# A four-layer graph network on one core: layer 3's first chunk moved into the last attention head

## The chip, the cores and the metric

The kernel runs on one core of a Trainium2 chip. Its time is the device time of one launch in microseconds (us); lower is better. A profiled execution gives, for every instruction, when it started, how long it was busy and what its engine had waited for. The engines are TensorE (PE; PEld is its weight load), VectorE (DVE), ScalarE (ACT), GpSimd (POOL) and SyncE (SP), whose queue issues most of the DMAs.

## The reference, cut to what matters

A graph of N = 2708 nodes with D = 512 features passes through four layers, each on the layer norm and relu of x, and each added to x. Layer 2 is attention with H = 8 heads of O = 64 outputs, and an elu behind it; layer 3 is a mean over neighbours.

```python
# layer 2, h = relu(layernorm(x))
Wh = einsum('nd,hdo->hno', h, W)
e = leaky_relu(f1[:, :, None] + f2[:, None, :], 0.2)
attention = softmax(where(adj > 0, e, NEG_INF), axis=-1)
x = x + elu(einsum('hnm,hmo->hno', attention, Wh))
# layer 3, h = relu(layernorm(x))
agg = mask @ h / maximum(deg, 1.0)
combined = concatenate([h @ W_self + b_self, agg @ W_nb + b_nb], axis=-1)
x = x + relu(combined @ W_comb + b_comb)
```

## The kernel before, in words

Nodes are cut into NC = 22 **chunks** of R = 128 rows (the last has 20). The two matrices of layer 3 are multiplied with W_comb beforehand (`fused`), so a chunk of layer 3 needs two products of 512 by 512: `nb3` (what the neighbours will be given, split into a high and a low half by `halves`) and `self3` (its own share plus a bias b3, sent to DRAM as s3). Then every chunk is summed over its neighbours (`aggregate`).

The attention runs as 220 **steps** in one loop. A step is one chunk of neighbours m for one head or half head ("unit"); the first and the last head are cut in two by columns, and the last unit covers columns 1408 to 2707. I number the 22 steps of this last unit 0 to 21; in the code they are steps 198 to 219. In a step s

- `make` (VectorE, L1066) writes the weights t of the step, 128 x 1300 here, into a tile "t2" (TILES = 4 buffers); the loop calls it three steps ahead;
- `scale` (ScalarE, L1051 and L1053) writes whs: the chunk's values wh and a column of ones, both times a factor of each row, also three steps ahead, in 4 buffers;
- `multiply` (TensorE, L1266) multiplies the two into "av" (eight matmuls) and "sums" (four).

After a unit, `evict` copies av and sums to SBUF (ScalarE) and to DRAM as avT and sumT (SP's queue). Layer 3 starts by reading them back. Its steps for a chunk c are

- `load3`: aT (256 KB) and sT (40 KB) from avT and sumT, and x2 (256 KB), all on SP's queue;
- `turn3`: a small product with `mix` and four transposes (TensorE), four 8-wide operations that end with a reciprocal (VectorE, L1221 to L1224), and y = av times the reciprocal, one 128 x 512 operation of VectorE (L1226);
- `elu3`: z = min(y, 0) (GpSimd, L1233), x + max(y, 0) (VectorE), tanh and exp of z (ScalarE, L1236 and L1237, with a table load between them), their product (VectorE, L1238), and its addition to x (VectorE, L1239);
- `save3`: x to DRAM on ScalarE's queue;
- `normalize3`: statistics of x (VectorE), a root (ScalarE, L223, with a table load), its reciprocal, and hn = (x - mean) * rs (VectorE, L234). `norm` has a second form, `scalar=True`, in which VectorE makes a one-element shift and ScalarE writes hn (L231);
- `transpose3`: four transposes of hn (TensorE, L245) and a relu to hT (ScalarE, L247);
- then `nb3` and `self3`.

The author plans what runs beside the attention with `behind(s, fn, c)`: fn is called at the end of step s. The tile framework then orders the instructions of each engine itself and puts in the waits; each engine executes its list strictly in that order. Before, the plan puts chunk 0's steps up to `transpose3` and parts of chunks 1 to 4 into steps 6 to 21 of the last unit; nb3 and self3 of all chunks follow after the loop:

```python
        for c in range(NC):
            nb3(c)
            if c:
                do(transpose3, c + 1)
            do(turn3, c + 3)
            do(normalize3, c + 2)
            do(save3, c + 2)
            do(elu3, c + 3)
            do(load3, c + 5)
            final = self3(c)
            if c == 0:
                transpose3(1)
```

Of the kernel before, what the change touches and what calls it, by code (L numbers as in the profile page):

```python
# [8 lines left out]
F32 = mybir.dt.float32  # L9
# [5 lines left out]
AF = mybir.ActivationFunctionType  # L15
ALU = mybir.AluOpType
# [4 lines left out]
P = 128  # L21

R = 128
# [3 lines left out]
TILES = 4  # L27
# [17 lines left out]
def fast_layers(  # L45
# [36 lines left out]
    nc = tc.nc  # L82
    N, D = x_in.shape
    H, _, O = w2.shape
    NC = -(-N // R)
# [6 lines left out]
    def rows(c):  # L92
        return min(R, N - c * R)

    def move(engine, dst, src):

        if dst.shape[0] == last_rows:
            cut = last_rows // 16 * 16
            engine.dma_start(dst[:cut], src[:cut])
            return engine.dma_start(dst[cut:], src[cut:])  # L100
        return engine.dma_start(dst, src)
# [21 lines left out]
    common = ctx.enter_context(tc.tile_pool(name="common", bufs=2))  # L123
# [84 lines left out]
    def any_product(c, po, lhsT, w, n):  # L208
        if c == NC - 1:
            product_of_last(po, lhsT, w)  # L210
        else:
            product(po, lhsT, w, n)
# [3 lines left out]
    def norm(xc, n, scalar=False):  # L216

        st = small.tile([P, nc.vector.BN_STATS_DIM], F32, name="ln_st")
        nc.vector.bn_stats(st[:n], xc[:n])  # L219
        mv = small.tile([P, nc.vector.BN_AGGR_DIM], F32, name="ln_mv")  # L220
        nc.vector.bn_aggr(mv[:n], st[:n])  # L221
        rs = small.tile([P, 1], F32, name="ln_rs")
        nc.scalar.activation(rs[:n], mv[:n, 1:2], AF.Sqrt, bias=eps[:n], scale=1.0)  # L223
        nc.vector.reciprocal(rs[:n], rs[:n])
        hn = common.tile([P, D], F32, name="hn", tag="t", bufs=3)
        if scalar:
            shift = small.tile([P, 1], F32, name="ln_shift")
            nc.vector.tensor_scalar(
                shift[:n], mv[:n, 0:1], rs[:n], -1.0, op0=ALU.mult, op1=ALU.mult
            )  # L230
            nc.scalar.activation(hn[:n], xc[:n], AF.Relu, bias=shift[:n], scale=rs[:n])  # L231
            return hn
        normed.append(
            nc.vector.tensor_scalar(  # L234
                hn[:n], xc[:n], mv[:n, 0:1], rs[:n], op0=ALU.subtract, op1=ALU.mult
            ).ins
        )
        return hn
# [89 lines left out]
    bias3 = dram.tile([1, D], F32, name="bias3")  # L328
# [641 lines left out]
    one6 = at.tile([R, S], F32, name="one6")  # L970
    nc.gpsimd.memset(one6, 0.0)
    nc.gpsimd.memset(one6[:, 6:7], 1.0)
    row, weight, wh, whs, acc, sides, made = {}, {}, {}, {}, {}, {}, []

    def load_row1(h, lo, hi):

# [79 lines left out]
    def make(s):  # L1056
        u, m = steps[s]
        h, lo, hi = units[u]
        q = rows(m)
        g, k = where[m]  # L1060
        if in_tails(u, m):
            weight[s] = tails_row[:LINES]
            made.append(made[-1])
            return
        t = at.tile([R, N], F32, name="t2", bufs=TILES)
        ins = nc.vector.scalar_tensor_tensor(  # L1066
            t[:q, : hi - lo],
            row[h][:q, lo:hi],
            ec[:q, m, h : h + 1],
            vT[g][:q, k, lo:hi],  # L1070
            op0=ALU.max,
            op1=ALU.mult,
        )
        weight[s] = t[:q]
        made.append(ins.ins)
# [114 lines left out]
    tails_w = tails.tile([P, len(middle), O + S], F32, name="tails_w")  # L1190
    nc.gpsimd.memset(tails_w, 0.0)
    tails_f = tails.tile([P, 3], F32, name="tails_f")
    kept3, l3_weights = {}, []


    def load3(c):
# [15 lines left out]
    def turn3(c):  # L1212
        xc, aT, sT = kept3[c]
        pr = ps.tile([P, 2, H], F32, name="sums_ps", tag="ps")
        nc.tensor.matmul(pr[:R], sT, mix[:NS], start=True, stop=True)
        pt = ps.tile([P, H, O], F32, name="av_ps", tag="ps")
        flat = pt.rearrange("p h o -> p (h o)")
        for k in range(NF):
            nc.tensor.transpose(flat[:R, k * P : (k + 1) * P], aT[:, k, :], ident)  # L1219
        rs = e3.tile([R, H, 1], F32, name="rs")  # L1220
        nc.vector.tensor_tensor(rs[:, :, 0], er[:, c], pr[:R, 0], ALU.mult)  # L1221
        nc.vector.tensor_tensor(rs[:, :, 0], rs[:, :, 0], pr[:R, 1], ALU.add)
        nc.vector.tensor_scalar(rs[:, :, 0], rs[:, :, 0], TINY, None, op0=ALU.max)
        nc.vector.reciprocal(rs[:, :, 0], rs[:, :, 0])  # L1224
        y = e3.tile([R, H, O], F32, name="y3")
        nc.vector.tensor_tensor(y, pt[:R], rs.to_broadcast([R, H, O]), ALU.mult)  # L1226
        kept3[c] = xc, y.rearrange("p h o -> p (h o)")

    def elu3(c):

        xc, y = kept3[c]
        z = e3.tile([R, D], F32, name="z3")
        nc.gpsimd.tensor_scalar(z, y, 0.0, None, op0=ALU.min)  # L1233
        nc.vector.scalar_tensor_tensor(xc[:R], y, 0.0, xc[:R], op0=ALU.max, op1=ALU.add)
        th = e3.tile([R, D], F32, name="th3", bufs=1)
        nc.scalar.activation(th, z, AF.Tanh, scale=0.5)  # L1236
        nc.scalar.activation(z, z, AF.Exp)  # L1237
        nc.vector.scalar_tensor_tensor(z, z, 1.0, th, op0=ALU.add, op1=ALU.mult)  # L1238
        nc.vector.tensor_tensor(xc[:R], xc[:R], z, ALU.add)  # L1239
        kept3[c] = xc  # L1240

    def save3(c):
        n = rows(c)
        move(nc.scalar, x3[c * R : c * R + n, :], kept3[c][0][:n])

    def normalize3(c):
        kept3[c] = kept3[c], norm(kept3[c], R)

    def transpose3(c):
        kept3[c] = kept3[c][0], relu_T(kept3[c][1], R)  # L1250
# [167 lines left out]
        behind(first + 2, count_neighbors, i)  # L1418

    for at_step, fn, c in (  # L1420
        (16, load3, 0),
        (15, load3, 1),
        (9, turn3, 0),
        (8, load3, 2),
        (8, elu3, 0),
        (6, normalize3, 0),
        (6, save3, 0),
        (6, turn3, 1),
        (5, load3, 3),
        (2, transpose3, 0),  # L1430
        (2, turn3, 2),
        (1, load3, 4),
    ):
        behind(len(steps) - at_step, fn, c)

    for s in range(len(steps)):
        if s == (len(units) - 3) * NC + 1:
            tails_ctx.close()
            e3_ctx = ctx.enter_context(ExitStack())
            e3 = e3_ctx.enter_context(  # L1440
                tc.tile_pool(name="e3", bufs=2, side="right", reuse_waits="tile")
            )
        if s + 6 < len(steps) and (s + 6) % NC % GROUP == 0:
            load_wh(s + 6)
        if s + 3 < len(steps):
            scale(s + 3)
            make(s + 3)
        if s + 1 < len(steps):
            compare(s + 1)
        multiply(s)  # L1450
        multiply_sides(s - 1)
        for fn, args in plan.pop(s, ()):
            if fn in (load_l3_weights, spread_nodes, split):
                with tc.issue_after(made[s]):
                    fn(*args)
            else:
                fn(*args)
# [4 lines left out]
    with ExitStack() as stack:  # L1462
        margin = stack.enter_context(tc.tile_pool(name="margin", bufs=1))
        margin.tile([P, 112], F32, name="margin")
        ring = stack.enter_context(tc.tile_pool(name="ring3", bufs=NC - 1, reuse_waits="tile"))
        b3 = ring.tile([P, D], F32, name="b3", bufs=1)
        nc.sync.dma_start(
            b3, bass.AP(tensor=bias3.tensor, offset=bias3.offset, ap=[[0, P], [1, D]])
        )
        h3 = {}  # L1470
        wself, wnb = l3_weights

        def nb3(c):
            pn = ps.tile([P, D], F32, name="nb3_ps", tag="ps")
            any_product(c, pn, kept3[c][1], wnb, R)
            h3[c] = halves(ring, pn, c)

        def self3(c):
            n = rows(c)
            po = ps.tile([P, D], F32, name="self_ps", tag="ps")  # L1480
            any_product(c, po, kept3.pop(c)[1], wself, R)
            y = common.tile([P, D], F32, name="y", tag="t", bufs=3)
            for own in corners if c == NC - 1 else [(slice(0, n), slice(0, D))]:
                ins = nc.vector.tensor_tensor(y[own], po[own], b3[own], ALU.add)
                move(nc.scalar, s3[c * R : c * R + n, own[1]], y[own])
            return ins.ins

        def do(fn, c):
            if c < NC:
                fn(c)  # L1490


        elu3(1)
        normalize3(1)
        save3(1)
        elu3(2)
        for c in range(NC):
            nb3(c)
            if c:
                do(transpose3, c + 1)  # L1500
            do(turn3, c + 3)
            do(normalize3, c + 2)
            do(save3, c + 2)
            do(elu3, c + 3)
            do(load3, c + 5)
            final = self3(c)
            if c == 0:
                transpose3(1)

        e3_ctx.close()  # L1510
        wk = stack.enter_context(
# [688 lines left out]
```

## Time and profile before

| what | us |
|---|---|
| median of 3 runs (1754.12 to 1757.56) | 1755.75 |
| the profiled execution's own time | 1757.88 |
| its span | 1756.1 |
| TensorE busy | 1728.0 |
| VectorE busy | 1307.0 |
| ScalarE busy | 850.1 |
| GpSimd busy | 248.0 |
| step 0 of the last unit starts on TensorE | 1315.7 |
| the last sums of the attention end | 1359.6 |
| nb3 of chunk 0 starts | 1359.5 |
| the last self3 ends and the aggregation begins, about | 1533 |

Times within the execution count from the start of the span. A line of the timeline gives start, duration, engine, line, operation, output<-inputs, shapes and count; a bracket at its end gives how long the engine was idle before it and which instruction ended that. TensorE's ends are modelled: a TensorE that is busy is not thereby at full speed, and the granted clock (1.00 is full) is read beside it.

### The profile page before, as it was taken

The numbers are of one execution on the slowest core, as the hardware profiler recorded it, in microseconds if no ns is written. First come the engines' busy times: TensorE is split into PE (matmuls) and PEld (weight loads), VectorE is DVE, ScalarE is ACT, GpSimd is POOL, SyncE is SP. The second block draws the span as 40 slices with busy tenths as digits, with TensorE's granted clock in tenths as the row PEclk, the third lists the DMA queues.
The fourth block names the chain that finished last, engine by engine and source line by source line (L and its number), as shares of the span: only waits on it lengthen the run. The fifth ranks groups of instructions, "written<-read, shape, count | busy, mean of one in ns | idle before, by whom it ended". The sixth has DMA issues, their size and how long they took to land.

```text
span 1756.1 us, 29494 instructions
## 1 busy us (share of the span) xinstructions
PE 1728.0 (98%) x11280; PEld 1050.8 (60%) x11280; DVE 1307.0 (74%) x1889; ACT 850.1 (48%) x1547; POOL 248.0 (14%) x252
## 2 busy tenths in 40 slices
PE   8999999999999999999999999999999999999998
PEld 5567777744468887644474554433434455588886
DVE  7759889855455557878699999999999777633334
ACT  5447777622210000365888888888794566400000
POOL 1003323311111112265000000000001222100000
PEclk9999999999999999999899999999999999999999
DMA  8436666444551112332420221122022444313221
GB/s 291 139 117 199 206 207 186 136 114 129 115 135 49 48 49 66 113 126 93 125 63 15 60 64 34 38 64 61 14 68 69 135 139 132 112 34 110 74 72 41
DMA packets 167227, 177.37 MB, mean 101 GB/s; under 512 B 84127, under 2 KB 106591, under 8 KB 166060
## 3 DMA queue, kind: packets, MB, share of 16 engines
q1 hardware_dynamic: 144428, 131.99, 27.1%
q10 hardware_dynamic: 18808, 33.37, 5.1%
q0 software_dynamic: 3840, 10.03, 1.5%
q8 instruction: 90, 1.47, 0.4%
q14 instruction: 61, 0.50, 0.1%
HBM read 111.64 MB, written 55.36 MB: 95 GB/s over the span
## 4 chain that ended last, share of the span: by engine, by line
PE 84%; DVE 9%; issue 2%; ACT 2%; DMA 1%; SPq 0%; POOL 0%; ACTq 0%; DVEq 0%; POOLq 0%
PE acc L424 36%; PE av L1266 15%; PE nb_ps L187 8%; DVE t L1066 6%; PE h_ps L187 4%; PE line_ps L187 4%; PE sums L1266 4%; PE self_ps L187 4%; PE hT_ps L245 2%; PE wh_ps L187 2%; PE fused_ps L370 2%; PE av_ps L1219 1%; PE adj_sums L1365 1%; ACT b L1084 1%; DVE kt L870 0%
## 5 line engine op out<-in xcount | busy, mean ns | idle before, releaser
L1066 DVE SCALAR_TENSOR_TENSOR t<-rb,ec,vT 128x2708 f32<-128x2708 f32 (+2 forms) x214 | 510.7, 2453 | 19.5 <-PE sums L1266 17.8
L1266 PE MATMUL av<-t,whs 128*32 128x451 f32 (+5 forms) x4432 | 431.1, 514 | 4.4 <-DVE t L1066 1.4
L424 PE MATMUL acc<-halves,kt 128*128 128x512 f32 x1848 | 426.4, 391 | 2.4 <-DVE kt L870 2.1
L424 PEld LDWEIGHTS acc<-halves,kt 128*128 128x128 f32 x1848 | 345.2, 188 | 79.8 <-DVE kt L870 6.8
L1084 ACT ACTIVATE b<-t,eb 128x2708 bf16<-128x2708 f32 (+1 forms) x119 | 285.0, 2395 | 36.6 <-DVE t L1066 36.2
L1266 PEld LDWEIGHTS av<-t,whs 128*32 128x32 f32 (+1 forms) x4432 | 168.1, 110 | 182.2 <-issue 145.4
L424 PE MATMUL acc<-halves,ar 128*128 128x512 f32 x924 | 243.6, 414 | 0.0
L424 PEld LDWEIGHTS acc<-halves,ar 128*128 128x128 f32 x924 | 172.6, 188 | 58.2 <-issue 20.8
L223 ACT ACTIVATE ln_rs<-ln_mv,eps 128x1 f32<-128x1 f32 x88 | 25.6, 294 | 306.4 <-DVE ln_mv L221 298.4
L870 DVE SCALAR_TENSOR_TENSOR kt<-lastr,index,vT 128x512 fp32r<-128x512 int16 (+3 forms) x154 | 112.6, 742 | 75.8 <-PE acc L424 75.4
L1517 DVE CAST kt<-vT 128x512 fp32r<-128x512 uint8 (+3 forms) x154 | 56.3, 368 | 131.2 <-PE acc L424 131.2
L1233 POOL TENSOR_SCALAR z<-y 128x512 f32<-128x512 f32 x22 | 44.1, 2003 | 647.1 <-DMA aT<-avT 522.8
L555 DVE TENSOR_TENSOR_SCAN cum<-ai,deg 128x512 int16<-128x512 int32 (+2 forms) x110 | 128.3, 1170 | 0.0
L598 ACT ACTIVATE cum<-cum,limit 128x512 int16<-128x512 int16 (+3 forms) x132 | 88.0, 667 | 51.9 <-DVE deg L563 49.7
L1051 ACT ACTIVATE whs<-wh,ef 128x64 f32<-128x64 f32 x214 | 72.7, 343 | 54.3 <-PE sums L1266 22.0
L219 DVE BATCH_NORM_STATS2 ln_st<-x 128x6 f32<-128x512 f32 x88 | 60.3, 687 | 47.7 <-DMA x<-x 33.3
L1266 PE MATMUL sums<-t,whs 128*32 128x325 f32 (+4 forms) x952 | 92.8, 451 | 0.0
L187 PE MATMUL nb_ps<-wfn,hT 128*128 128x512 f32 x168 | 78.1, 609 | 2.1 <-ACT hT L247 2.1
L187 PE MATMUL h_ps<-w0s,hT 128*128 128x512 f32 x168 | 76.5, 598 | 0.0
L187 PE MATMUL wh_ps<-w2s,hT 128*128 128x512 f32 x168 | 75.9, 594 | 0.3 <-ACT hT L247 0.3
L549 ACT ACTIVATE ar<-ai 128x512 fp32r<-128x512 int32 (+2 forms) x132 | 75.0, 568 | 1.5 <-DMA ai<-in_adj 1.0
L187 PE MATMUL nb_ps<-wn,hT 128*128 128x512 f32 x168 | 75.6, 592 | 0.0
(210 smaller groups left out, 1908.2 us busy)
## 6 DMA issues: line engine op xcount, KB each, us to landing
x<-x SPq DMA_DIRECT2D x105, 256.0 KB
ai<-in_adj SPq DMA_DIRECT2D x84, 256.0 KB
x<-x ACTq DMA_DIRECT2D x84, 256.0 KB
x<-in_x SPq DMA_DIRECT2D x42, 256.0 KB
rb<-rT SPq DMA_DIRECT2D x7, 1354.0 KB
wh<-whd SPq DMA_DIRECT2D x63, 96.0 KB
packed<-two POOLq DMA_DIRECT2D x44, 128.0 KB, 3.2
whd<-wh SPq DMA_DIRECT2D x21, 256.0 KB
```

Of the source, the lines that this page charges most:

```text
L187: nc.tensor.matmul(po[:n], lhsT[:, f, :n], w[:, f, :], start=(f == 0), stop=(f == NF - 1))
L219: nc.vector.bn_stats(st[:n], xc[:n])
L424: nc.tensor.matmul(acc[:R], weight[:, k * R : (k + 1) * R], parts[:, i, :], start=(m == 0 and i == 0), stop=(m == NC - 1),)
L549: nc.scalar.activation(ar[:, :gw], ai[:, :gw], AF.Square, accum_out=squares[:R, m, g : g + 1])
L555: nc.vector.tensor_tensor_scan(cum[:n, :gw], ai[:n, :gw], ai[:n, :gw], 0.0 if g == 0 else deg[:n, m : m + 1], op0=ALU.add, op1=ALU.max,)
L598: nc.scalar.activation(cum[:n, :gw], cum[:n, :gw], AF.Sign, bias=limit[:n], scale=-1.0, accum_out=signs[:n, m, g : g + 1],)
L870: nc.vector.scalar_tensor_tensor(by_chunk(kt, cs), lastr[:, cs[0] * R : (cs[-1] + 1) * R].rearrange("p (c r) -> p c r", r=R), index[:R, m ...
L1051: nc.scalar.activation(t[:q, :O], wh.pop((u, m))[:q], AF.Copy, scale=by)
L1066: ins = nc.vector.scalar_tensor_tensor(t[:q, : hi - lo], row[h][:q, lo:hi], ec[:q, m, h : h + 1], vT[g][:q, k, lo:hi], op0=ALU.max, op1=AL ...
L1084: nc.scalar.activation(b[:q, : hi - lo], weight[s][:, : hi - lo], AF.Sigmoid, bias=eb[:q, m, h : h + 1], scale=STEEP,)
L1266: nc.tensor.matmul(p[j * S : (j + 1) * S, : b - a], lhsT, rhs[:, part * size + a : part * size + b], start=(s % NC == 0), stop=(s % NC == ...
L1517: nc.vector.tensor_copy(by_chunk(kt, cs), pattern(m, cs))
```

## The change

Seven things are done at once.

- In the last unit two steps share one tile: an even step takes a new tile "t2" and its second half is kept for the odd step behind it.
- The plan of layer 3 inside the attention starts at step 2 (`len(steps) - 20`) instead of step 6, and reaches further: chunk 0 through nb3 and self3, chunk 1 through transpose3, chunk 2 through normalize3, chunk 3 through elu3, and the load of chunk 5.
- For chunks 0 and 1 (EASED), y is written by ScalarE in eight pieces of 128 x 64, the last addition of elu3 is GpSimd's, and hn is ScalarE's.
- tanh's output moves from a buffer of its own to the common tag "t", which hn and y of self3 use too.
- nb3 and self3 are defined earlier, and chunk 0's halves have a pool of their own (first3), made during the seventh head; the ring of the others has one buffer less.
- The bias b3 is loaded at that point too.
- The loop after the attention starts at chunk 1, and the calls ahead of it are gone.

```diff
-        t = at.tile([R, N], F32, name="t2", bufs=TILES)
+        if u < len(units) - 1:
+            t = at.tile([R, N], F32, name="t2", bufs=TILES)
+        elif m % 2 == 0:
+            t = at.tile([R, N], F32, name="t2", bufs=TILES)
+            second[0] = t[:, hi - lo :]
+        else:
+            t = second[0]
...
+    EASED = 2
...
         y = e3.tile([R, H, O], F32, name="y3")
-        nc.vector.tensor_tensor(y, pt[:R], rs.to_broadcast([R, H, O]), ALU.mult)
+        if c < EASED:
+            for h in range(H):
+                nc.scalar.activation(y[:, h], pt[:R, h], AF.Copy, scale=rs[:, h])
+        else:
+            nc.vector.tensor_tensor(y, pt[:R], rs.to_broadcast([R, H, O]), ALU.mult)
...
-        th = e3.tile([R, D], F32, name="th3", bufs=1)
+        th = common.tile([P, D], F32, name="th3", tag="t", bufs=3)[:R]
...
-        nc.vector.tensor_tensor(xc[:R], xc[:R], z, ALU.add)
+        eng = nc.gpsimd if c < EASED else nc.vector
+        eng.tensor_tensor(xc[:R], xc[:R], z, ALU.add)
...
-        kept3[c] = kept3[c], norm(kept3[c], R)
+        kept3[c] = kept3[c], norm(kept3[c], R, scalar=c < EASED)
...
     for at_step, fn, c in (
-        (16, load3, 0),
-        (15, load3, 1),
-        (9, turn3, 0),
-        (8, load3, 2),
-        (8, elu3, 0),
-        (6, normalize3, 0),
-        (6, save3, 0),
-        (6, turn3, 1),
-        (5, load3, 3),
-        (2, transpose3, 0),
-        (2, turn3, 2),
-        (1, load3, 4),
+        (20, load3, 0),
+        (19, load3, 1),
+        (16, turn3, 0),
+        (16, elu3, 0),
+        (15, load3, 2),
+        (13, normalize3, 0),
+        (13, save3, 0),
+        (12, turn3, 1),
+        (11, load3, 3),
+        (11, transpose3, 0),
+        (10, elu3, 1),
+        (9, nb3, 0),
+        (8, self3, 0),
+        (7, normalize3, 1),
+        (7, save3, 1),
+        (6, turn3, 2),
+        (5, load3, 4),
+        (5, transpose3, 1),
+        (4, elu3, 2),
+        (2, turn3, 3),
+        (1, normalize3, 2),
+        (1, save3, 2),
+        (1, elu3, 3),
+        (1, load3, 5),
     ):
         behind(len(steps) - at_step, fn, c)
...
-        elu3(1)
-        normalize3(1)
-        save3(1)
-        elu3(2)
-        for c in range(NC):
+        for c in range(1, NC):
             nb3(c)
-            if c:
-                do(transpose3, c + 1)
+            do(transpose3, c + 1)
...
-            if c == 0:
-                transpose3(1)
```

More of the change, by code (lines that the diff above doesn't have):

```diff
@@ L972, in fast_layers @@
     nc.gpsimd.memset(one6[:, 6:7], 1.0)
-    row, weight, wh, whs, acc, sides, made = {}, {}, {}, {}, {}, {}, []
+    row, weight, wh, whs, acc, sides, made, second = {}, {}, {}, {}, {}, {}, [], {}
     def load_row1(h, lo, hi):
@@ L1192, in fast_layers @@
     tails_f = tails.tile([P, 3], F32, name="tails_f")
-    kept3, l3_weights = {}, []
+    kept3, h3, l3_weights = {}, {}, []
+    EASED = 2
     def load3(c):
@@ L1244, in save3, with nb3, self3 @@
         move(nc.scalar, x3[c * R : c * R + n, :], kept3[c][0][:n])
+    def nb3(c):
+        pn = ps.tile([P, D], F32, name="nb3_ps", tag="ps")
+        any_product(c, pn, kept3[c][1], l3_weights[1], R)
+        h3[c] = halves(rings3[min(c, 1)], pn, c)
+    def self3(c):
+        n = rows(c)
+        po = ps.tile([P, D], F32, name="self_ps", tag="ps")
+        any_product(c, po, kept3.pop(c)[1], l3_weights[0], R)
+        y = common.tile([P, D], F32, name="y", tag="t", bufs=3)
+        for own in corners if c == NC - 1 else [(slice(0, n), slice(0, D))]:
+            ins = nc.vector.tensor_tensor(y[own], po[own], b3[own], ALU.add)
+            move(nc.scalar, s3[c * R : c * R + n, own[1]], y[own])
+        return ins.ins
     def normalize3(c):
-        kept3[c] = kept3[c], norm(kept3[c], R)
+        kept3[c] = kept3[c], norm(kept3[c], R, scalar=c < EASED)
     def transpose3(c):
@@ L1438, in fast_layers @@
             tails_ctx.close()
+            first3 = ctx.enter_context(
+                tc.tile_pool(name="first3", bufs=1, side="right", reuse_waits="tile")
+            )
+            rings3 = [first3]
+            b3 = first3.tile([P, D], F32, name="b3")
+            nc.sync.dma_start(
+                b3, bass.AP(tensor=bias3.tensor, offset=bias3.offset, ap=[[0, P], [1, D]])
+            )
             e3_ctx = ctx.enter_context(ExitStack())
@@ L1464, in fast_layers @@
         margin.tile([P, 112], F32, name="margin")
[L1465 to L1486, printed above, removed]
+        ring = stack.enter_context(tc.tile_pool(name="ring3", bufs=NC - 2, reuse_waits="tile"))
+        rings3.append(ring)
         def do(fn, c):
```

## The prediction

> **What bounds the kernel now.** I read the chain of work that ended last first.
>
> ```profile
> PE 84%; DVE 9%; issue 2%; ACT 2%; DMA 1%; SPq 0%; POOL 0%; ACTq 0%; DVEq 0%; POOLq 0%
> ```
>
> TensorE carries it, so a gain has to be TensorE time that is idle or slow at the place of the change. Next come stretches around the hand-over from the last half head to layer 3 (columns: busy us of each engine with instructions in brackets, granted clock, DMA share, GB/s).
>
> ```profile
> 1315.70:1339.00 23.30, 23.30 (x344) 11.01 (x341) 23.30 (x16) 9.63 (x33) 0.00 (x0) 1.00 0.26 62
> 1339.00:1350.80 11.80, 11.80 (x160) 5.76 (x156) 9.86 (x17) 5.41 (x14) 2.67 (x1) 1.00 0.26 67
> 1350.80:1357.50 6.70, 3.75 (x49) 2.24 (x50) 5.53 (x13) 4.04 (x6) 1.93 (x1) 1.00 0.18 52
> 1357.50:1364.30 6.80, 6.80 (x26) 2.60 (x15) 5.75 (x9) 4.25 (x8) 2.45 (x2) 0.50 0.59 156
> 1364.30:1372.20 7.90, 5.80 (x22) 2.85 (x21) 5.12 (x14) 3.81 (x6) 1.72 (x1) 1.00 0.67 194
> 1372.20:1396.20 24.00, 24.00 (x79) 12.37 (x80) 17.50 (x41) 14.36 (x19) 5.48 (x3) 1.00 0.37 114
> ```
>
> TensorE never idles before 1350.8 or after 1372.2. Between them it idles 2.95 + 2.10 us, and runs 6.8 us at half clock, which is 3.4 us of work lost. So the hand-over costs 5.05 + 3.4 = **8.5 us**; nothing else is there to win. TensorE's timeline says who is late:
>
> ```profile
> 1351.94 1.30 PE L1266 MATMUL av<-t,whs 128*32 128x325 f32 x16 [1.13 <-DVE ln_mv L221]
> ...
> 1355.62 0.63 PE L245 MATMUL hT_ps<-ident,hn 128*128 128x128 f32 x4 [1.83 <-DVE hn L234]
> ...
> 1359.54 6.07 PE L187 MATMUL nb_ps<-wfn,hT 128*128 128x512 f32 x8
> ...
> 1372.19 3.70 PE L187 MATMUL nb_ps<-wfn,hT 128*128 128x512 f32 x8 [2.10 <-ACT hT L247]
> ```
>
> The third row is chunk 0's product at half clock (6.07 us; the same eight take 3.60 or 3.70 elsewhere). ScalarE shows what a chunk's elu does to a queue in order:
>
> ```profile
> 1342.03 0.31 ACT L1053 ACTIVATE whs<-one,ef 128x32 f32<-128x32 f32 x1
> 1345.26 0.63 ACT L1236 ACTIVATE th<-z 128x512 f32<-128x512 f32 x1 [2.92 <-POOL z L1233]
> 1345.80 0.33 ACT L1051 ACTIVATE whs<-wh,ef 128x64 f32<-128x64 f32 x1
> 1346.14 1.28 ACT L1237 ACT_TABLE_LOAD   x1
> 1347.44 0.63 ACT L1237 ACTIVATE z<-z 128x512 f32<-128x512 f32 x1
> 1347.97 0.30 ACT L1053 ACTIVATE whs<-one,ef 128x32 f32<-128x32 f32 x1
> ```
>
> The tanh waits for GpSimd's minimum, and the scaled weights (whs) that TensorE needs for its next attention steps stand behind it. VectorE makes the weights t without a gap:
>
> ```profile
> 1283.79 57.09 DVE L1066 SCALAR_TENSOR_TENSOR t<-rb,ec,vT 128x1408 f32<-128x1408 f32 x37
> ```
>
> **Two rules of the skill.** The Trainium skill, "TensorE: Matmul & The Clock Gate", Part 1 (the HAM clock gate), says that an idle window of about 3.4 us halves the clock, that a busy window restores it, and that the windows run freely. The trace agrees on the size (0.50 for 6.8 us, two windows) but not on the trigger: gaps of 1.13 and 1.83 us together sufficed, while 2.10 us at 1370 did not close the gate. I go by the trace: some 1.5 us idle in one window closes it. "ScalarE: Activation LUTs", Rules for kernel authors, gives 0.3 us for an activation plus 0.83 ns an element, 0.353 us for 64 columns, and 2.7 us for a table switch. The page's 128x64 row has 343 ns, which agrees; but the next one starts about 0.25 us later (1341.77 to 1342.03), and the switch above took 1.30 us from start to start. I go by the trace.
>
> **The change, part by part.** Steps 0 to 21 are those of the last half head; TensorE starts step 0 at 1315.7 and takes 1.643 us a step, VectorE one t each 1.484 us from 1314.1. The order of instructions in the changed program, as built, carries the argument.
>
> *Half tiles in one buffer: 0.* They let VectorE run up to eight half tiles ahead instead of four. VectorE had no idle at all in these steps, so no buffer held it. The cover is its own rate: from a level start it gains only 0.16 us a step. If a write of one half were ordered behind reads of the other, TensorE could start a step one t later; VectorE's lead of a step or more hides that.
>
> *Memory and DMA: 0.* The bias load moves from 1362.7 into the seventh head on SP's queue (0.35 us there, no one behind it is due). aT and sT of chunks 0 and 1 pass one load of wh on SP; that load goes out near 1323.5 instead of 1321.0 and is scaled after 1333. The first aT and sT must land for a transpose at 1327.5 instead of 1339.1. The DMAs fall silent at 1328 in this trace and chunk 0's are the older, so 0 to 0.5 us, inside the wait of step 14 below. tanh's output sharing the tag "t" makes hn, th, y take three buffers in turn, each free a chunk (7.9 us) later: 0.
>
> *Moved work, sums.* VectorE loses two 512-wide multiplies, two additions (0.69 each) and two hn (0.55) and gains two one-element steps: about -3.8 us. ScalarE gains 16 pieces x 0.245 and two hn x 0.81 (row L231): 5.5 us. GpSimd gains two additions, 1.65 each (row L1113, 128x512). TensorE gains nothing: 2 x 3.43 us of products of chunk 0 only move. So the whole matter is where TensorE waits, and I walk it.
>
> VectorE's order has the makes of steps 0 to 12, then chunk 0's four 8-wide steps between the next makes. The last, the reciprocal, ends at 1314.1 + 16 x 1.484 + 4 x 0.12 = 1338.4. ScalarE's pieces of y for chunk 0 stand before the whs of step 14: 1338.5 + 8 x 0.245 + 0.1 = 1340.6; that whs at 1340.9. TensorE is due at step 14 at 1315.7 + 14 x 1.643 + two turns of 0.7 = 1340.1 to 1340.4: **idle 0.5**. GpSimd's minimum, 2.00 (row L1233): 1342.65. ScalarE: tanh, table, exp end at 1342.7 + 0.53 + 1.29 + 0.63 = 1345.1; the whs of step 15 stand behind all three: 1345.4. TensorE ended step 14 at 1342.6: **idle 2.9**. Behind exp: VectorE's product 0.69 (1345.9), GpSimd's addition 1.65 (1347.6), statistics 0.69 and 0.17 (1348.5). Then VectorE's order has both last makes, 2 x 1.484, and only then the reciprocal and shift of the norm: 1351.85. ScalarE meanwhile holds the save of chunk 0 until 1347.6, the first piece of chunk 1, a table load, the root, seven pieces and one whs (0.25 + 1.29 + 0.30 + 7 x 0.245 + 0.25 behind 1348.5): 1352.3. hn 0.81: 1353.1. The transposes of chunk 0 stand in TensorE's order inside step 16, reached at 1348.4: **idle 4.8**. After that the products of chunk 0, steps 17 to 21 and chunk 1 follow with about 0.4 of waits in two places, since hn of chunk 1 is made while the products run. Late next, but hidden by those 6.9 us: chunk 1's th, hT and save. Sum of idle: about **8.6 us**, against 5.05.
>
> The clock: both long gaps leave more than 1.5 us idle in a window whatever its phase, so TensorE resumes at half speed. From 1353.1 it is dense; release takes the rest of a window and a whole one, 3.4 to 6.8 us, mean 5.1, and half of that is lost: 1.7 to 3.4, taken **2.5**. Before lost 3.4.
>
> Total: 8.6 + 2.5 - 8.5 = **+2.6 us**. The profiled execution took 1757.9 us (span 1756.1), so it would take 1760.5; the median shown is 1755.75, 2.1 us less, and from it the forecast is **1758.3 us**, +0.15%, which is inside the 0.2% (3.5 us) that a measurement can tell from no change.
>
> Bounds of what is not shown: a piece from PSUM with its scale from memory, 0.20 (less than the fastest pair) to 0.345 us (none overlaps): 15 of them stand ahead of hn, so -0.7 to +1.5. GpSimd's addition beside VectorE: 1.28 (row L855) to 2.58 (slowest of L1113): -0.4 to +0.9. Its first minimum, 2.00 or 2.67 as here at 1342.6: 0 to +0.7. Clock -0.8 to +0.9 (2.6 if a third window passes). Ends together: about 0.7 to 6.6 us over before; before's own clock loss, by phase, may be 2 us larger, which lowers the low end to -1.3.
>
> **Rivals.** *Slower, ScalarE's queue.* The pieces don't overlap: at 0.345 each the whs of steps 14 to 18 and hn stand 1.5 us later, giving +4.1, **1759.9**, and up to 1761.5 with a slow GpSimd. It decides from 0.31 us a piece (0.9 us over 15). For: PSUM source and a scale read per piece. Against: 128x64 with such a scale paces at 0.25.
> *Faster.* The products cover the hand-over, TensorE waits nowhere: all 8.5 us, **1747.3**; half of it 1751.5. For: chunk 1's norm then has 6.9 us of cover, and the 2.10 at 1372 goes. Against: the built order puts y behind 16 makes, and two whs groups behind the tanh.
> *A swap.* The gaps only change places and the gate closes once on either side, with phases that cost before as much: **1755.75**.
>
> **How the numbers follow.** Forecast 0.55, swap 0.07: within 0.2%, 0.62. ScalarE's queue 0.30: slower. Faster 0.08. The range leaves out the faster case and the last of the slow one: 1753.5 (low end -1.3 and the runs' own spread of 1.6 below the median) to 1762.5.
>
> **What would show it.** After: chunk 0's nb_ps near 1355.5, before the last sums; gaps of about 0.5, 2.9 and 4.8 us ahead of whs steps 14 and 15 and of the first hT_ps; ScalarE's th waiting 1.7 us for GpSimd; clock 0.50 for 3 to 7 us after 1353; no gap before chunk 1's nb_ps; its start near 1373.5. y pieces pacing over 0.31 us prove the slower rival. Wrong altogether if hT_ps comes before 1350 (y not behind the makes), or if the first turn waits for its aT.

## The result, and the profile after

The changed kernel takes **1764.96 us** (median of 6 runs, 1761.26 to 1767.29) against 1756.69 (6 runs, 1754.12 to 1757.56): ratio **1.0048**, 95% interval 1.0036 to 1.0059. It is slower by 8.3 us; the forecast was 1758.3, which is 2.6 above the median of 1755.75 that it started from, and its range ended at 1762.5. The profiled execution took 1765.07 us, its span is 1763.3 (before 1756.1).

The chain that ended last holds less TensorE than before:

```profile
PE 71%; DVE 11%; issue 10%; ACT 3%; DMA 3%; SPq 0%; POOL 0%; ACTq 0%; DVEq 0%; POOLq 0%
```

Most of its "issue" is no loss: 116.6 us are one piece, from 1222.8 to 1339.4 inside the attention, where TensorE is busy for 115.8 us at full clock. The loss shows from 1390 to 1500: there the chain of the kernel before is TensorE's alone, and of that of the changed one TensorE has about 4%; over half is VectorE's, the rest mostly ScalarE's and a load of x (see below).

I cut the time at the start of chunk 2's nb3, where the moved work is over in both kernels. From step 0 of the last half head to there, the kernel before takes 64.49 us (1315.72 to 1380.21) and the changed one 67.11 (1315.00 to 1382.11): **+2.6**, the sum that was forecast. From there to the aggregation's first matmul it is 152.91 (to 1533.12) against 158.04 (to 1540.15): **+5.1**. Together +7.7; step 0 starts 0.7 earlier and the aggregation is 0.2 longer, which gives the span's +7.2.

**The hand-over.** Stretches of the changed kernel (columns as in the prediction):

```profile
1315.00:1341.90 26.90, 26.89 (x380) 12.80 (x376) 26.87 (x25) 10.13 (x37) 2.48 (x1) 1.00 0.32 77
1341.90:1346.50 4.60, 1.19 (x20) 0.61 (x24) 2.44 (x4) 3.44 (x7) 1.19 (x2) 1.00 0.00 0
1346.58:1349.99 3.41, 3.41 (x29) 1.22 (x18) 2.25 (x5) 1.11 (x4) 1.85 (x1) 0.50 0.19 76
1350.48:1357.50 7.02, 3.85 (x29) 1.63 (x29) 3.50 (x6) 6.98 (x20) 2.13 (x2) 0.76 0.14 41
1353.41:1356.82 3.41, 3.17 (x20) 1.50 (x24) 0.24 (x1) 3.38 (x7) 1.32 (x1) 0.50 0.29 84
1357.50:1374.10 16.60, 16.60 (x139) 7.77 (x135) 8.00 (x22) 7.67 (x13) 3.03 (x2) 1.00 0.31 89
```

The idle time lies in two stretches, and behind each of them the clock falls to half for 3.41 us (the third and the fifth row). TensorE's timeline names the gaps; at half clock, eight pieces of sums take 1.18 us in place of 0.73:

```profile
1345.32 1.30 PE L1293 MATMUL av<-t,whs 128*32 128x325 f32 x16 [3.42 <-ACT whs L1051]
1346.44 1.18 PE L1293 MATMUL sums<-t,whs 128*32 128x325 f32 x8
...
1353.65 1.11 PE L245 MATMUL hT_ps<-ident,hn 128*128 128x128 f32 x4 [3.17 <-ACT hn L231]
```

ScalarE shows the queue ahead of them: eight pieces of y in 1.75 us, tanh waiting 2.69 us for GpSimd, the whs of the next step behind the exp, and hn behind the save, the root and the second chunk's pieces. VectorE's part of that norm stands behind its last two makes at the same time (its shift ends at 1352.62), as the prediction had it.

```profile
1337.57 1.75 ACT L1235 ACTIVATE y<-av_ps,rs 128x64 f32<-128x64 f32 x8 [4.15 <-DVE rs L1231]
...
1342.45 0.63 ACT L1247 ACTIVATE th<-z 128x512 f32<-128x512 f32 x1 [2.69 <-POOL z L1244]
1343.10 1.28 ACT L1248 ACT_TABLE_LOAD   x1
1344.39 0.63 ACT L1248 ACTIVATE z<-z 128x512 f32<-128x512 f32 x1
1344.93 0.33 ACT L1051 ACTIVATE whs<-wh,ef 128x64 f32<-128x64 f32 x1
...
1348.46 0.35 ACTq L101 DMA_DIRECT2D x<-x  x1
...
1350.93 0.29 ACT L223 ACTIVATE ln_rs<-ln_mv,eps 128x1 f32<-128x1 f32 x1
1351.13 1.52 ACT L1235 ACTIVATE y<-av_ps,rs 128x64 f32<-128x64 f32 x7
...
1352.75 0.85 ACT L231 ACTIVATE hn<-x,ln_shift,ln_rs 128x512 f32<-128x512 f32 x1
```

**The rest of layer 3.** From chunk 4 to chunk 19, nb3 starts 8.20 us after that of the chunk before (8.27 for chunk 3); in the kernel before it was 7.92. TensorE's timeline marks no gap, but the transposes start 3.66 us behind nb3's start instead of 3.43, so that is where it is held. VectorE shows what changed; this is one chunk of the kernel before (L234 is hn, L1238 is z times tanh, L1239 its addition to x, L1226 y of the next turn):

```profile
1403.36 0.64 DVE L234 TENSOR_SCALAR hn<-x,ln_mv,ln_rs 128x512 f32<-128x512 f32 x1
...
1405.95 0.69 DVE L1238 SCALAR_TENSOR_TENSOR z<-z,th 128x512 f32<-128x512 f32 x1 [1.09 <-ACT z L1237]
1406.68 0.69 DVE L1239 TENSOR_TENSOR x<-x,z 128x512 f32<-128x512 f32 x1
...
1408.83 0.15 DVE L1221 TENSOR_TENSOR rs<-er,sums_ps 128x8 f32<-128x8 f32 x1
...
1409.75 0.69 DVE L1226 TENSOR_TENSOR y<-av_ps,rs 128x512 f32<-128x512 f32 x1
1410.48 0.69 DVE L1234 SCALAR_TENSOR_TENSOR x<-y,x 128x512 f32<-128x512 f32 x1
```

And one chunk of the changed kernel (L1249 is z times tanh, L1251 its addition, L1237 y of the next turn):

```profile
1401.64 0.55 DVE L234 TENSOR_SCALAR hn<-x,ln_mv,ln_rs 128x512 f32<-128x512 f32 x1
...
1403.06 0.16 DVE L1228 TENSOR_TENSOR rs<-er,sums_ps 128x8 f32<-128x8 f32 x1 [0.28 <-PE sums_ps L1222]
...
1404.00 0.69 DVE L1237 TENSOR_TENSOR y<-av_ps,rs 128x512 f32<-128x512 f32 x1
1404.72 0.69 DVE L1245 SCALAR_TENSOR_TENSOR x<-y,x 128x512 f32<-128x512 f32 x1
1405.33 1.10 DVE L1249 SCALAR_TENSOR_TENSOR z<-z,th 128x512 f32<-128x512 f32 x1
1406.35 0.68 DVE L299 TENSOR_TENSOR halves<-nb_ps,halves 128x512 fp32r<-128x512 f32 x1
1406.95 0.67 DVE L1251 TENSOR_TENSOR x<-x,z 128x512 f32<-128x512 f32 x1
...
1409.64 0.16 DVE L224 RECIPROCAL ln_rs<-ln_rs 128x1 f32<-128x1 f32 x1 [1.07 <-ACT ln_rs L223]
1409.84 0.55 DVE L234 TENSOR_SCALAR hn<-x,ln_mv,ln_rs 128x512 f32<-128x512 f32 x1
```

TensorE's and ScalarE's part of the same chunk (changed kernel):

```profile
1402.24 0.65 PE L245 MATMUL hT_ps<-ident,hn 128*128 128x128 f32 x4
1402.73 0.29 PE L1222 MATMUL sums_ps<-mix,sT 80*128 80x16 f32 x2
...
1410.44 0.66 PE L245 MATMUL hT_ps<-ident,hn 128*128 128x128 f32 x4
```

```profile
1407.66 0.33 ACTq L101 DMA_DIRECT2D x<-x  x1
1408.02 1.28 ACT L223 ACT_TABLE_LOAD   x1 [3.03 <-DVE x L1251]
1409.31 0.30 ACT L223 ACTIVATE ln_rs<-ln_mv,eps 128x1 f32<-128x1 f32 x1
```

The same operations stand in another order. In the kernel before, one chunk's product with tanh and its addition come first and the next chunk's turn behind them; in the changed kernel the turn comes first. That closes a ring. The transposes (TensorE, 1402.24) are followed by the turn's sums (1402.73), these release rs (1403.06), y, x, then z, the halves, the addition to x (1406.95); ScalarE's save of x waits for it, and behind it stand the table load (1408.02) and the root (1409.31); reciprocal, hn (1409.84), and the next transposes at 1410.44. Step by step 0.49 + 0.33 + 0.94 + 0.72 + 0.61 + 1.02 + 0.60 + 1.07 + 1.29 + 0.33 + 0.20 + 0.60 = 8.20 us: the ring, not TensorE, sets the pace. In the kernel before, hn ends at 1404.00 and its transposes start at 1407.40, when TensorE reaches them, 3.4 us later. In some chunks the profile's chain goes from hn to a load of x (issued at 1402.21) and on to L1245; but L1245 starts 0.72 or 0.73 us behind y in all ten chunks from 1404 to 1479, as in the kernel before (0.73), so that load held nothing up.

One link is stretched: L1249 takes 1.10 us, where the same operation took 0.69 before. GpSimd's minimum runs beside it in the changed kernel (1404.77 to 1406.76) and had ended in the one before. The Trainium skill, "SBUF — State Buffer", section "SBUF: two separate sides", calls the port pair of VectorE and GpSimd an exclusive lock that an operation with two SBUF inputs needs, the loser blocking fully. The row agrees that there is a price (0.41 us), and not that it is a full block, since L1249 ended 0.33 us before GpSimd did. Without these 0.41 us the ring would take 7.79, less than TensorE's 7.92. By that estimate, which no run isolates, the order costs time here because it also brings this product beside the minimum.

### The profile page after: what moved, and what is told of

Same layout as the page of the kernel before. It is cut to its first block, busy times and chain, and to the rows that moved or that the text cites. A ratio compares the mean times of both kernels' runs of the same rounds, so it can differ in the third digit from the quotient of the medians.

```text
span 1763.3 us, 29467 instructions
## 1 busy us (share of the span) xinstructions
PE 1733.0 (98%) x11280; PEld 1050.7 (60%) x11280; DVE 1312.3 (74%) x1885; ACT 855.2 (48%) x1567; POOL 251.9 (14%) x254
## 4 chain that ended last, share of the span: by engine, by line
PE 71%; DVE 11%; issue 10%; ACT 3%; DMA 3%; SPq 0%; POOL 0%; ACTq 0%; DVEq 0%; POOLq 0%
PE acc L424 36%; PE av L1293 12%; DVE t L1072 5%; PE nb_ps L187 5%; PE h_ps L187 4%; PE line_ps L187 4%; PE sums L1293 3%; PE hT_ps L245 2%; PE wh_ps L187 2%; PE fused_ps L370 2%; DMA x<-x 1%; DVE z L1249 1%; ACT L223 1%; DVE x L1245 1%; DVE x L1251 1%
## 5 line engine op out<-in xcount | busy, mean ns | idle before, releaser
L1293 PE MATMUL sums<-t,whs 128*32 128x325 f32 (+4 forms) x952 | 96.6, 453 | 0.0
L187 PE MATMUL self_ps<-wfs,hT 128*128 128x512 f32 x168 | 75.6, 592 | 0.0
```

What stands on the lines that cost most here:

```text
L187: nc.tensor.matmul(po[:n], lhsT[:, f, :n], w[:, f, :], start=(f == 0), stop=(f == NF - 1))
L1293: nc.tensor.matmul(p[j * S : (j + 1) * S, : b - a], lhsT, rhs[:, part * size + a : part * size + b], start=(s % NC == 0), stop=(s % NC == ...
```

## The experiments

Theory A: the order of VectorE's list in the loop, as the program is built, sets the pace of layer 3, and the shared tag is what changed that order. Its rivals: B, the moved hand-over and the new pools set the pace; C, the common tag's three buffers make the loop wait whatever the order. Each ratio is to runs of the kernel before on the same chip; "hand-over" is step 0 to nb3 of chunk 2, "rest" from there to the aggregation, both of the profiled execution.

| run | median us | ratio (95%) | hand-over | rest |
|---|---|---|---|---|
| before | 1755.7 to 1756.7 | | 64.49 | 152.91 |
| changed | 1764.96 | 1.0048 (1.0036 to 1.0059) | 67.11 | 158.04 |
| 1 before, tanh in the tag | 1763.99 | 1.0048 (1.0034 to 1.0062) | 67.77 | 158.20 |
| 2 changed, tanh over y | 1762.57 | 1.0034 (1.0021 to 1.0046) | 70.74 | 152.91 |
| 3 run 2, nothing eased | 1768.79 | 1.0068 (1.0054 to 1.0082) | 65.32 | 165.08 |
| 4 run 2, whole tiles | 1768.61 | 1.007 (1.0056 to 1.0084) | 63.97 | 165.21 |
| 5 own tanh buffer in the loop | 1765.1 | 1.0047 (1.0033 to 1.0061) | 68.42 | 157.78 |
| 6 run 5, whole tiles | 1761.49 | 1.0024 (1.0015 to 1.0032) | 64.43 | 157.80 |
| 7 run 6, over y in the attention | 1758.88 | 1.0016 (1.0009 to 1.0023) | 63.73 | 156.64 |
| 8 before, half tiles | 1761.19 | 1.003 (1.0018 to 1.0042) | 69.65 | 152.91 |
| 9 changed, elu3 first | 1760.42 | 1.0024 (1.0014 to 1.0034) | 69.77 | 152.91 |
| 10 run 1, elu3 first | 1762.59 | 1.0034 (1.0022 to 1.0046) | 70.53 | 152.91 |
| 11 chunk 0 later | 1755.14 | 0.9992 (0.9984 to 1.0) | 62.39 | 152.91 |
| 12 run 11, addition on VectorE | 1750.71 | 0.9973 (0.9961 to 0.9984) | 59.14 | 152.91 |

**1. The tag alone, in the kernel before.**

```diff
-        th = e3.tile([R, D], F32, name="th3", bufs=1)
+        th = common.tile([P, D], F32, name="th3", tag="t", bufs=3)[:R]
```

> The kernel before with one edit: tanh's output goes to the common tag t (three buffers, shared with hn and y) instead of a buffer of its own. Theory A (the shared tag makes the built order of VectorE in layer 3 put a chunk's statistics and norm behind the next chunk's turn, and closes a loop that is longer than TensorE's 7.92 us a chunk): chunks of layer 3 start 8.2 us apart, +0.28 for some 17 chunks, so 4 to 6 us over before, 1761 to 1762.5. Theory B (the slower chunks come from the hand-over or the moved pools, the tag is free): 7.92 us a chunk, 1756 to 1757.

This one line costs as much as the whole change, and the pace is 8.20 from chunk 3 on, with VectorE's list in the changed kernel's order. B falls. The hand-over also grew by 3.3 us, which I had not expected: 1.2 of it lie between the nb3 of chunks 0 and 1, and 1.7 between those of chunks 1 and 2.

**2. The changed kernel without the tag.**

```diff
-        th = common.tile([P, D], F32, name="th3", tag="t", bufs=3)[:R]
+        th = y
```

> The changed kernel with tanh's output written over y, whose last reader is done by then, so that it neither takes the tag t nor a buffer of its own. Theory A: chunks 7.92 us apart again, 4 to 6 us under the changed kernel, and the hand-over's +3 stays: 1758.5 to 1761. Theory B: still 8.2 a chunk, 1764 to 1766.

The pace is back at 7.92, but chunk 2's nb3 starts 12.31 us after chunk 1's: in the built order two elus stand ahead of chunk 2's norm there.

**3 and 4. The same with nothing eased, and the same with whole tiles.**

```diff
-    EASED = 2
+    EASED = 0
```

> As the kernel with tanh over y, and EASED = 0: y, the last addition and hn of chunks 0 and 1 stay on VectorE. If ScalarE's pieces and GpSimd's addition make the hand-over's gaps (0.5, 3.4, 3.2 and half clock), they shrink: ScalarE's queue is shorter by 8 pieces ahead of whs, y by some 1.4 us and the addition by 2 us, so 2 to 4 us less than with EASED = 2, 1755 to 1758. If the gaps come from where the makes and the tanh stand in the orders, about the same, within 1.5 us.

```diff
-        if u < len(units) - 1:
-            t = at.tile([R, N], F32, name="t2", bufs=TILES)
-        elif m % 2 == 0:
-            t = at.tile([R, N], F32, name="t2", bufs=TILES)
-            second[0] = t[:, hi - lo :]
-        else:
-            t = second[0]
+        t = at.tile([R, N], F32, name="t2", bufs=TILES)
```

> As the kernel with tanh over y, with a whole tile for each step (four of them). If the half tiles are worth nothing: within 1 us of it. If they let VectorE's order put the makes of steps 12 to 15 and 18 to 21 ahead of chunk 0's small operations and so delay it: 1 to 3 us faster; if four tiles make VectorE wait for TensorE: slower by as much.

The times missed what was expected of both, since the pace is 8.64 us. The loop has a third order, with three of the next turn's four 8-wide operations ahead of the product with tanh; ScalarE's list differs there too (tanh ahead of the root), so the price is that of both lists. Tanh's buffer is the same as in run 2, so the pace goes with the order and not with the buffer; and the product (L1243 of run 4) takes 0.68 us, so this order is slow without a stretched one:

```profile
1408.25 0.17 DVE L1224 TENSOR_SCALAR rs<-rs 128x8 f32<-128x8 f32 x1
1408.33 0.68 DVE L1243 SCALAR_TENSOR_TENSOR z<-z,y 128x512 f32<-128x512 f32 x1
```

The hand-over of run 3 is 5.4 us shorter than that of run 2, that of run 4 6.8; 4.2 and 4.3 us of it are the late chunk of run 2, which neither has.

**5 to 7. A buffer of its own for the loop only.** The memory for one is free only behind the attention, so there the tag (5 and 6) or y (7) is used; 6 and 7 have whole tiles.

```diff
         rings3.append(ring)
+        own_th.append(stack.enter_context(tc.tile_pool(name="own_th", bufs=1, reuse_waits="tile")))
...
-        th = common.tile([P, D], F32, name="th3", tag="t", bufs=3)[:R]
+        th = own_th[0].tile([R, D], F32, name="th3") if own_th else common.tile([P, D], F32, name="th3", tag="t", bufs=3)[:R]
```

> The changed kernel, but tanh's output uses the common tag only for the chunks inside the attention; in the loop behind it, it has a buffer of its own again. VectorE's built order in the loop is then the old one (x before the row sums' reciprocals of the next turn, z first). Theory A (the order of VectorE's list in the loop, which the shared tag changes, sets the pace of layer 3): chunks 7.92 us apart, hand-over as in the changed kernel (about +3 us), so 1759 to 1760.5. Theory B (the new pools and the moved hand-over set the pace, or the tag's buffers inside the attention do): 8.20 us apart, 1764 to 1766.

> As the run with its own tanh buffer in the loop, but with a whole tile for every step of the last half head. Theory A: 7.92 us apart, and the hand-over as short as in the earlier run without half tiles (step 0 to chunk 2's product 64.0 us, the kernel before 64.5): 1755.5 to 1757. If half tiles don't matter for the hand-over: like the run with them, 1759 to 1760.5. Theory B: 8.20 or more, over 1762.

> As the run before it, but inside the attention tanh's output is written over y instead of into the common tag. VectorE's built order in the loop is the other one that ran at 7.92. Theory A: 7.92 us apart again although the order inside the attention differs, 1755.5 to 1758. Theory B: the pace follows what is done inside the attention, so another pace than the run before it.

All three run at 7.92 after chunk 3 or 4, and all three are slower than A said, by one late chunk each: 12.79, 12.81 and 11.66 us instead of 7.92. (Run 5's median lies in B's range; its pace does not.) There the list goes over from one order to the other. ScalarE of run 7 shows it:

```profile
1385.79 0.63 ACT L1242 ACTIVATE th<-z 128x512 f32<-128x512 f32 x1 [4.25 <-POOL z L1239]
1386.45 0.63 ACT L1243 ACTIVATE z<-z 128x512 f32<-128x512 f32 x1
1387.10 1.28 ACT L223 ACT_TABLE_LOAD   x1
1388.39 0.30 ACT L223 ACTIVATE ln_rs<-ln_mv,eps 128x1 f32<-128x1 f32 x1
...
1389.51 0.29 ACT L223 ACTIVATE ln_rs<-ln_mv,eps 128x1 f32<-128x1 f32 x1
```

A chunk's root waits until the next chunk's elu is through, and then two roots follow each other. Such a place costs 3.7 to 4.9 us once; A had left it out.

**8. Half tiles alone, in the kernel before** (the lines of run 4 the other way round).

> The kernel before with one part alone: half tiles in the last half head. VectorE's built order in the loop stays as before. The prediction's step (half tiles cost 0, VectorE's own rate is the cover): 1756 to 1757. The rival: half tiles let VectorE run further ahead and put chunk 0's small operations behind more makes, so layer 3 starts later: 1758 to 1760. Pace 7.92 in either case.

They cost 4.8 us, more than the rival said, all of it in the hand-over. VectorE runs its makes in one piece (the last thirteen are the first row), and chunk 0's 8-wide operations, which started at 1340.81 in the kernel before, stand behind them, at 1343.37; their reciprocal ends at 1345.5 instead of 1341.6:

```profile
1324.08 19.36 DVE L1072 SCALAR_TENSOR_TENSOR t<-rb,ec,vT 128x1300 f32<-128x1300 f32 x13
1343.37 0.14 DVE L1227 TENSOR_TENSOR rs<-er,sums_ps 128x8 f32<-128x8 f32 x1
```

**9 and 10. Two calls swapped where they are written.** In 9 the plan's last entries are swapped likewise; 10 is run 1 with the swap in the loop.

```diff
+            do(elu3, c + 3)
             do(normalize3, c + 2)
             do(save3, c + 2)
-            do(elu3, c + 3)
```

> The changed kernel with two calls swapped where they are written: elu3 of the next chunk ahead of normalize3 and save3, in the plan's last entries and in the loop. The shared tag, half tiles and everything else stay. In VectorE's built order tanh's product and its addition then stand ahead of the next turn's reciprocals in every chunk, as before, and no chunk's two norms stand side by side. Theory A (the order alone sets the pace, the shared buffer itself costs nothing): 7.92 us a chunk with the changed kernel's hand-over, 1765.0 - 17 x 0.28 = 1760.2, say 1759 to 1761. Theory C (the shared tag's buffers make the loop wait, whatever the order): 8.20 us a chunk, 1764 to 1766.

> The kernel before with tanh's output in the common tag (which alone cost 7.6 us) and elu3 written ahead of normalize3 in the loop. VectorE's built order is the old one from the loop's second chunk on; once, at the norms of chunks 2 and 3, two norms stand side by side behind two elus. Theory A: 7.92 us a chunk; the place with two norms may cost up to 4 us once, so 1757 to 1763, with the gap in one place. Theory C: 8.20 us a chunk, 1763 to 1765.

With the tag still shared and the list again in the first order, both run at 7.92. C falls: the chain of run 9 from 1390 to 1500 is TensorE's alone again, so the buffers themselves hold up nothing that counts. Run 9's median met the number of A, but not by its reckoning alone: its rest is 5.1 us shorter than the changed kernel's, and its hand-over 2.7 longer (1.17 of it idle ahead of chunk 2's transposes). VectorE of run 9, where the product with tanh (L1249) is ahead of y of the next turn (L1237) and takes 0.69 us:

```profile
1403.33 0.69 DVE L1249 SCALAR_TENSOR_TENSOR z<-z,th 128x512 f32<-128x512 f32 x1 [1.35 <-ACT z L1248]
...
1404.73 0.68 DVE L1251 TENSOR_TENSOR x<-x,z 128x512 f32<-128x512 f32 x1
...
1407.13 0.69 DVE L1237 TENSOR_TENSOR y<-av_ps,rs 128x512 f32<-128x512 f32 x1
```

Run 10 has its changeover at chunk 2, which keeps it near the upper end of its range.

**11 and 12. Towards a faster one.** Run 11 is run 4 with chunk 0's products later in the plan; run 12 also takes chunk 1's addition from GpSimd.

```diff
-        (11, transpose3, 0),
+        (5, transpose3, 0),
...
-        (9, nb3, 0),
-        (8, self3, 0),
+        (5, nb3, 0),
+        (4, self3, 0),
...
-        (5, transpose3, 1),
+        (3, transpose3, 1),
...
-        (1, normalize3, 2),
-        (1, save3, 2),
+        (2, normalize3, 2),
+        (2, save3, 2),
```

> The changed kernel with whole tiles, tanh written over y, and a later plan: chunk 0's transposes, nb3 and self3 and chunk 1's transposes some two to three attention steps later in TensorE's list, chunk 2's norm a step earlier. The built order in the loop is one that ran at 7.92. If the hand-over's loss is only TensorE standing in its list ahead of hn (4.4 us of idle in the run with whole tiles), the later place fills it with attention steps: 1756.4 - 0.5 - 4.4 = 1751.5, say 1750.5 to 1753.5, and no idle above 1 us before 1370. If the products are then late for chunk 1 or the wait goes to another place in the list: 1755 to 1757.

The gap of 4.4 us ahead of the transposes is gone (1.10 us are left ahead of an earlier step), but a new wait took most of the gain. On ScalarE, hT stood behind the save of chunk 1's x, and that save waited for GpSimd's addition. First TensorE, then ScalarE of run 11:

```profile
1355.63 3.70 PE L187 MATMUL nb_ps<-wfn,hT 128*128 128x512 f32 x8 [3.15 <-ACT hT L247]
```

```profile
1354.58 0.35 ACTq L101 DMA_DIRECT2D x<-x  x1
1354.98 0.60 ACT L247 ACTIVATE hT<-hT_ps 128x512 f32<-128x512 f32 x1 [1.92 <-POOL x L1245]
```

```diff
-        eng = nc.gpsimd if c < EASED else nc.vector
+        eng = nc.gpsimd if c < 1 else nc.vector
...
-        (5, nb3, 0),
+        (4, nb3, 0),
...
-        (3, transpose3, 1),
+        (2, transpose3, 1),
```

> The run with chunk 0's products later, with chunk 1's addition to x on VectorE instead of GpSimd, nb3 of chunk 0 one plan step later and chunk 1's transposes one later. In that run TensorE stood 3.15 us ahead of chunk 0's nb3, because hT waited on ScalarE behind the save of chunk 1's x, and that save for GpSimd's addition; in the built order hT now stands ahead of the save. If that wait is the cause: a gap of 1.0 to 2.1 us there (ScalarE's exp and last whs end near 1353), no new one, 1753 to 1754.3. If GpSimd's addition was not the cause, the gap stays at 3 us: 1755 to 1756.

TensorE of run 12 waits 1.10 and 1.09 us in all, and the clock stays at 1.00:

```profile
1341.11 1.30 PE L1287 MATMUL av<-t,whs 128*32 128x325 f32 x16 [1.10 <-DVE rs L1224]
...
1350.77 3.70 PE L187 MATMUL nb_ps<-wfn,hT 128*128 128x512 f32 x8 [1.09 <-ACT hT L247]
```

At 1750.71 us it beats the kernel before by 0.27% (0.16 to 0.39) and the changed one by some 14 us. It did better than expected; 2.6 us of its profiled execution are an earlier step 0 (1313.12 against 1315.72), which no part of the edit explains; over all fourteen traces it starts between 1313.0 and 1315.9, at 1313.38 in run 1 with its one line. The hand-over itself is 5.4 us shorter than before.

## Why the prediction was wrong, by its own steps

- **Memory, tanh in the tag "t": forecast 0, measured +5.1 us** in the rest of layer 3 (158.04 against 152.91), and 7.6 us in all when done alone (run 1). This is the step that failed. I asked only whether a buffer comes free in time. That was true, and run 9, with the tag still shared, runs at 7.92. What the runs show in its place is a ring of 8.20 us a chunk, longer than TensorE's 7.92. I did not ask what the shared buffer does to the built order, and compared the lists only up to the hand-over. The loop's list of VectorE, which the built program shows as well, had changed; every instruction that the loop issues should have been walked once around. Why the tag leads to another order stays open beyond run 9: with the same tag, the order of two calls in the source decides it.
- **Half tiles: forecast 0, measured +4.8 alone** (run 8), and 4.0 off the hand-over when they go (run 6 against run 5). I looked for a wait on a buffer. Their price is that VectorE's list can hold more makes ahead of chunk 0's small operations. The walk of the hand-over followed that list, so this cost stood in its sum, under another name.
- **The gaps: 0.5, 2.9 and 4.8 forecast, none, 3.42 and 3.17 measured**, 6.6 instead of 8.2. tanh waited 2.69 us, not 1.7, since GpSimd's first minimum took 3.00 us (2.00 taken; the bound of 2.67 was too low) and its first addition 2.60 (1.65 taken; bound 2.58). y, at 1.75 us for eight pieces, is 0.3 faster than taken. TensorE, at half clock behind the first gap, reached the transposes at 1350.5 and not at 1348.4, so part of the last gap became lost clock.
- **The clock: 2.5 forecast, 3.3 measured.** The forecast counted one fall, behind both gaps. There were two of 3.41 us, one behind each gap: half of the 3.41 and of the 3.17 us worked in them, 1.7 + 1.6.
- **TensorE gains nothing: about 1 us too low.** Less its gaps and lost clock, the hand-over takes 64.49 - 5.06 - 3.4 = 56.0 us before, 67.11 - 6.6 - 3.3 = 57.2 after, and 59.14 - 2.2 = 56.9 in run 12, which lost no clock. A likely reason, which no run isolates, is that the moved turns and products break up the attention's steps more often.
- **Their sum, +2.6, was met by luck** (67.11 - 64.49): the idle time was 2.0 too high (8.6 with its small waits, against 6.6), the clock 0.8 and TensorE's own time 1.2 too low. What was right: no gap ahead of chunk 1's nb3, and its start (1374.09, forecast 1373.5); chunk 0's came at 1357.50 (1355.5).
- **The rivals.** ScalarE's queue is refuted in its price: the pieces pace at 0.21 us, not 0.31 or more. The faster case did not come, and needed what runs 11 and 12 did: chunk 0's transposes behind more attention steps. None of the rivals looked beyond the hand-over.

## What to carry to other kernels

Where a scheduler lays out the lists, a shared buffer that never makes anyone wait can still cost, because it changes the order: compare the built order of every loop that touches it, not only the place of the change. Then walk one pass of the loop around: an operation on the ring hn, transposes, sums, reciprocals, y, addition, root costs time in every pass once the ring takes longer than the bound engine's own pass (8.20 against 7.92 us here), and the same operation off the ring costs none. And when work is moved ahead of a bound engine's wait, look for what else stands in that list: run 11 lost most of its 4.4 us to one save that waited for GpSimd.

## What the hardware showed that I had not expected

- The prediction's rule, some 1.5 us idle in one window halves the clock, does not hold as a rule. Wherever the clock is halved in the hand-over of the fourteen traces, it is for 3.41 or 6.83 us, so I count windows of 3.41 us from these changes (TensorE's ends are modelled, so the idle times are rough). The window ahead of a fall is idle for 1.53 us in the kernel before, and for 2.15 and 2.93 in the changed one; the gap of 2.10 us is split into 1.07 and 1.03 and halves nothing. So far the rule holds. But windows with 1.84 (run 4, 1338.43 to 1341.84) and 1.87 (run 6, 1340.07 to 1343.48) are not followed by half clock, and the gap of 3.15 us in run 11, which gives 1.45 and 1.70 when the windows are counted on from its last change at 872.65, leaves the clock at 1.00. The length of these windows, and that they run freely, are what the Trainium skill, "TensorE: Matmul & The Clock Gate", Part 1, has (about 3.4 us); what decides besides the idle time, no run here settles.
- GpSimd's first 128x512 minimum took 3.00 us in the changed kernel, where it started 1.03 us before VectorE ended a make, and 1.98 in runs 11 and 12, where it started 0.5 us ahead of two makes; there these took 3.40 us instead of 2.99. In these rows the operation that starts second is the one that loses. In the kernel before it took 2.67 with 1.31 us of a make left, so what is left of the make is not the whole price.
